# An expert queue of 71 blocks: the 38 behind the first 33 put in order by group instead of by expert

## The chip, the cores and the metric

The program runs on one core of a Trainium2 chip. A core has five engines that run at the same time, each with its own queue of instructions, taken strictly in the order written: TensorE (PE, matrix products), VectorE (DVE), ScalarE (ACT), GpSimd (POOL) and SyncE (SP, which here only starts transfers). Transfers between the on-chip memory and DRAM are started from the queues of SP, ACT and POOL and then run beside the engines. An instruction that starts a transfer waits at the head of its queue until the data that it needs are there, and everything behind it in that queue waits too. The metric is the device time of one execution in microseconds (us). "By over 0.2%" means, for this kernel, over 3.3 us.

## The reference, cut to what matters

Four layers run one after another on 64 sequences of 64 tokens, each a vector of 128 numbers: two cross-attention blocks, a gated fusion and a third attention block. The last one ends in a mixture of experts, the part that the change touches:

```python
h = _ln(x, ln_g, ln_b)
logits = h @ rw.T + rb
vals, idx = jax.lax.top_k(logits, K)          # K = 2 of E = 8 experts for each token
gates = jax.nn.softmax(vals, axis=-1)
h1 = gelu(einsum('nd,efd->enf', hf, fc1_w) + fc1_b)     # 128 -> 512
eo = einsum('enf,edf->end', h1, fc2_w) + fc2_b          # 512 -> 128
mixed = (eo[idx_f, n, :] * gates_f[..., None]).sum(axis=1)
return x + mixed
```

So each of the 4096 tokens needs the results of two experts, weighted by two gates, on top of its own row `x`.

## The kernel before, in words

**Groups.** The 4096 tokens are handled as eight groups of 512 (`NG = 8`, T = 512). A group passes through the layers as a Python generator, and `drive` (L152) interleaves the generators of several groups. The expert work, `experts` (L691), is one more generator, advanced between the others. A scheduler then fixes one order of instructions for each engine; nothing is reordered at run time.

**Router and scatter.** When a group's last attention is done, `router` (L1426) picks two experts for each token and scatters the token's row (with its number) to its place in `hrows`, a DRAM array with one region for each expert. This is 8 indirect transfers a group from POOL's queue. Region e holds the rows of expert e in the order of the groups, packed without gaps. `before` is the count of rows so far for each expert; the count after the last group of each part is kept in `endbase` (L1477, L1563).

**Blocks.** 128 rows of one region are a block, the unit of the expert queue. `PARTS = (5, 3)` splits the groups in two parts. The first part of the queue has `NSLOT[0]` = 33 blocks (L34), which are full when five groups have been routed. The second has 38. `table(h)` (L721), for the second part 34 small DVE instructions, works out on the chip which expert and which rows each block of part h has. `table(1)` walks two runs over the eight experts: first the blocks begun by the first five groups and not yet taken, then the rest. So by block 47 (`EARLY`, L35) all rows of groups 0 to 4 are done, and the blocks from 47 on have rows of groups 5, 6 and 7, expert by expert.

**One block.** `load` (L822, SP) fetches 128 rows and needs a table entry, read into a register of SP; the buffers of the rows are eight. `turn` (L844) transposes them on PE (tile `xt`) and copies them on ACT (tile `vp`); DVE works out where the result goes (`m`, `tob`). `stage_weights` (L836) copies the first weights of the block's expert on DVE (`h<-fcw`). `first` (L861) is four products on PE and the Gelu on ACT. `second` (L881) is four products on PE, one addition on DVE that takes the result out of PSUM (`km<-f,km`, called **y(i)** for block i below), and an indirect transfer on POOL that writes the rows to `yrows`. All PSUM tiles of these steps share seven buffers (`psm`).

**Sums.** `read(g)` (L909) fetches the two results of each token of a group, 256 KB each: the first (`s<-yrows`) from SP's queue, the second (`pT<-yrows`) from ACT's. A read waits for the landing of every result that may hold rows of its group. `summed(g)` (L927) is eight DVE instructions (`o<-s,gate,x` and `o<-pT,gate,o`) and one write of 256 KB from SP (`out<-o`); the tile `o` has two buffers.

**Order around the change.** The loop at L958 handles block after block: in turn t it writes `first(t)`, `second(t-2)`, `load(t+6)`, `stage_weights(t+1)` and `turn(t+2)`. L971 to L977 put in a read of groups 0 to 4 every fourth turn, the first three blocks after block 47's, each sum two turns behind its read. Groups 5, 6 and 7 are read and summed behind the last block (L979 to L985), with all three reads ahead of the first sum.

Of the kernel before, what the change touches and what calls it, by code (L numbers as in the profile page):

```python
# [13 lines left out]
ALU = mybir.AluOpType  # L14
AX = mybir.AxisListType
# [19 lines left out]
EARLY = ALL[0] + NE - 1  # L35
# [62 lines left out]
def kernel(ctx: ExitStack, tc: tile.TileContext, a: dict, out: bass.AP):  # L98
# [592 lines left out]
    def experts():  # L691
# [18 lines left out]
        def sums(nb, n, name):  # L710

            for step in (1, 2, 4, 8)[: 3 + (n > 8)]:
                more = wtile([P, 3 * NE], f"cum{step}", 1)
                nc.vector.memset(more[:, 0:NE], 0.0)
                nc.vector.tensor_tensor(
                    more[:, NE : NE + n], nb[:, NE : NE + n], nb[:, NE - step : NE - step + n], ALU.add
                )
                nb = more
            return nb[:, NE : NE + n]

        def table(h):  # L721

            ns = NSLOT[h]
            cnt = full[h] = wtile([P, NE], f"cnt{h}", 1)
            nc.vector.tensor_tensor(cnt, endbase[h], start, ALU.subtract)
            eb = wtile([P, ns], f"eb{h}", 1)
            if h == 0:
                nb = wtile([P, 3 * NE], "nb0", 1)
# [15 lines left out]

                taken = tables["taken"] = wtile([P, NE], "taken", 1)
                nc.vector.tensor_scalar(taken, cum, -1.0, float(ns), ALU.mult, ALU.add)
                nc.vector.tensor_tensor(taken, taken, whole, ALU.add)
                nc.vector.tensor_scalar(taken, taken, 0.0, None, ALU.max)
                nc.vector.tensor_tensor(taken, taken, whole, ALU.min)
                begun = tables["begun"] = wtile([P, NE], "begun", 1)  # L750
                nc.vector.tensor_reduce(begun, blocks_of(0, ALU.is_gt, 0), axis=AX.X, op=ALU.add)
            else:


                taken, begun = tables["taken"], tables["begun"]
                nb = wtile([P, 3 * NE], "nb1", 1)
                nc.vector.memset(nb[:, 0:NE], 0.0)
                at = wtile([P, 2 * NE + 1], "runs", 1)
                nc.vector.tensor_tensor(nb[:, NE : 2 * NE], begun, taken, ALU.subtract)
                late = nb[:, 2 * NE : 3 * NE]  # L760
                nc.vector.tensor_reduce(late, blocks_of(1, ALU.is_gt, 0), axis=AX.X, op=ALU.add)
                nc.vector.tensor_tensor(late, late, begun, ALU.subtract)
                cum = sums(nb, 2 * NE, "cum")
                yield
                nc.vector.scalar_tensor_tensor(
                    at[:, 0:NE], start, 1.0 / P, taken, op0=ALU.mult, op1=ALU.add
                )
                nc.vector.scalar_tensor_tensor(
                    at[:, NE : 2 * NE], start, 1.0 / P, begun, op0=ALU.mult, op1=ALU.add
                )  # L770
                nc.vector.memset(at[:, 2 * NE :], float(NE * REGION))
                step = wtile([P, 2 * NE], "step", 1)
                nc.vector.tensor_tensor(step, at[:, 1:], at[:, 0 : 2 * NE], ALU.subtract)
                nc.vector.tensor_tensor(step, step, nb[:, NE:], ALU.subtract)
                counts = wtile([P, 512], "pT", 7)
                ebs, rbs = ([counts[:, (2 * n + k) * ns : (2 * n + k + 1) * ns] for k in range(2)] for n in range(2))
                rb = counts[:, 4 * ns : 5 * ns]
                for k in range(2):
# [4 lines left out]
                    nc.vector.tensor_reduce(ebs[k], past, axis=AX.X, op=ALU.add)  # L783
                    if k == 0:

                        nc.vector.scalar_tensor_tensor(
                            eb, past[:, :, NE - 1 : NE].rearrange("p i e -> p (i e)"), -float(NE), ebs[0],
                            op0=ALU.mult, op1=ALU.add,
                        )
                    nc.vector.tensor_tensor(past, past, mid(step[:, ks], ns), ALU.mult)  # L790
                    nc.vector.tensor_reduce(rbs[k], past, axis=AX.X, op=ALU.add)
                yield
                nc.vector.tensor_tensor(eb, eb, ebs[1], ALU.add)
                nc.vector.tensor_tensor(rb, rbs[0], rbs[1], ALU.add)
                nc.vector.scalar_tensor_tensor(rb, rb, at[:, 0:1], index[:, 0:ns], op0=ALU.add, op1=ALU.add)
# [18 lines left out]
            tables[h] = tab, eb, hb  # L814

# [63 lines left out]
        results = [[] for _ in range(NH)]  # L879

        def second(i):  # L881
# [15 lines left out]
            late = i >= EARLY  # L897
            tc.add_to_no_dep_group("results", st.ins)
            if late:
                tc.add_to_no_dep_group("results1", st.ins)  # L900
            if i:
                tc.declare_no_dep(st.ins, group="results", reason="each row has one writer")
            if late and early_reads:
                tc.declare_no_dep(st.ins, group="reads0", reason="no rows of the first part in late blocks")
            results[late].append(st.ins)

        early_reads = []

        def read(g):  # L909

            h = PLACE[g][0]
            ys = []
            for k in range(2):
# [3 lines left out]
                if h == 0:  # L917
                    tc.add_to_no_dep_group("reads0", ld.ins)
                    early_reads.append(ld.ins)
                    if results[1]:  # L920
                        tc.declare_no_dep(ld.ins, group="results1", reason="no rows of the first part in late blocks")
                for st in sum(results[: h + 1], []):
                    tc.add_manual_dep(ld.ins, st.name, LANDED, reason="all results are in place")
# [715 lines left out]
```

## Time and profile before

| what | us |
|---|---|
| median of three runs | 1660.57 |
| lowest, highest | 1658.11, 1660.71 |
| the profiled execution | 1656.37 |
| its span, first to last instruction | 1654.6 |
| outside the span (difference) | 1.8 |

Times inside the kernel below are microseconds from the start of this span. The page gives the busy time of each engine and the groups of instructions; an instruction is named by its tiles, as output<-inputs, and nearly all carry the line L77, a helper through which every instruction is issued. So the reading goes by tiles. In a list of instructions by time, the number in brackets is how long the engine was idle ahead of the instruction, with what ended the wait. The granted clock is the share of full speed that TensorE was given.

| stretch of the span | what runs there |
|---|---|
| up to about 1488 | the layers, group by group |
| 1488 to 1520 | first expert blocks, beside the last scatters of rows on POOL |
| 1520 to 1637 | the rest of the 71 blocks, one every 1.9 us |
| 1637 to 1654.6 | last results land; groups 5, 6, 7 are read, summed and written |

### The profile page before, as it was taken

Reading aid. Unit: us, or ns where it says so; the run is one execution under the profiler, and the core shown is the slowest. Engines: PE = TensorE matmul, PEld = TensorE weight load, DVE = VectorE, ACT = ScalarE, POOL = GpSimd, SP = SyncE. Lnnn points to the kernel's source line nnn. Section 1 sums busy time; section 2 is a strip of 40 time slices with the busy share of each in tenths; the row PEclk is TensorE's granted clock in tenths of the full one; section 3 lists DMA queues with packets and bytes.
Section 4 is the critical chain, followed back from the end, with each engine's and each line's share of the span. In section 5 each row is a group of like instructions: output and inputs, shape, how many; then the busy total and the mean of one; then the engine's idle time right before and its main releaser. Section 6 shows DMA issues by size and latency. Waiting matters only on the chain.

```text
span 1654.6 us, 45059 instructions
## 1 busy us (share of the span) xinstructions
PE 1524.2 (92%) x17469; PEld 1132.4 (68%) x17469; DVE 1166.5 (70%) x3226; ACT 992.8 (60%) x2711; POOL 888.3 (54%) x852
## 2 busy tenths in 40 slices
PE   6999999999999999978888999989989899868995
PEld 4666666666666666646666676666767667668995
DVE  4767686867677677758897688676776688756555
ACT  4666455555655565535776565656777777427774
POOL 2546373645555564666887576644332223367543
PEclk9999999999999999979999899898999899759998
DMA  6776544545455554241001000000000000113244
GB/s 171 157 172 160 141 138 127 136 132 144 121 144 132 144 135 107 56 140 34 12 15 31 24 24 20 9 8 8 2 2 15 21 2 7 35 54 86 74 116 125
DMA packets 215540, 131.40 MB, mean 79 GB/s; under 512 B 38416, under 2 KB 201490, under 8 KB 215328
## 3 DMA queue, kind: packets, MB, share of 16 engines
q1 hardware_dynamic: 186016, 90.52, 22.9%
q10 hardware_dynamic: 24992, 29.54, 5.7%
q0 software_dynamic: 4320, 8.47, 1.5%
q8 instruction: 139, 2.28, 0.6%
q14 instruction: 73, 0.60, 0.1%
HBM read 66.48 MB, written 62.47 MB: 78 GB/s over the span
## 4 chain that ended last, share of the span: by engine, by line
PE 65%; DVE 18%; ACT 6%; POOL 6%; DMA 3%; issue 2%; SPq 0%; ACTq 0%; DVEq 0%; POOLq 0%
PE av L77 8%; PE psv L77 8%; PE proj L77 7%; PE psk L77 6%; PE f L77 6%; PE pt L77 6%; PE tok L77 5%; DVE mx L77 4%; PE pbd L77 4%; DVE s L77 4%; PE psc L77 4%; PE acc L77 3%; PE tr L77 2%; ACT z L77 2%; PE sc L77 2%
## 5 line engine op out<-in xcount | busy, mean ns | idle before, releaser
L77 ACT ACTIVATE s<-s,nm 128x128 f32<-128x128 f32 x512 | 198.1, 388 | 236.8 <-DVE nm L77 220.5
L77 POOL TENSOR_TENSOR s<-s,sm 128x512 f32<-128x512 f32 x128 | 130.4, 1040 | 208.7 <-DVE sm L77 208.7
L77 PE MATMUL pt<-ident,s 128*128 128x128 f32 x1536 | 213.0, 282 | 19.3 <-DVE s L77 12.1
L77 POOL TENSOR_TENSOR s<-s,mx 128x512 f32<-128x512 f32 x160 | 164.4, 1046 | 99.8 <-DVE mx L77 93.6
L77 PEld LDWEIGHTS pt<-ident,s 128*128 128x128 f32 x1536 | 177.0, 145 | 41.2 <-issue 17.7
L77 POOL TENSOR_TENSOR skew<-skew,mb 128x512 f32<-128x512 f32 x128 | 159.9, 1270 | 70.7 <-DMA skew<-scr 70.2
L77 ACT ACTIVATE pT<-pt 128x512 f32<-128x512 f32 x256 | 140.5, 600 | 79.6 <-PE pt L77 71.3
L77 POOL TENSOR_TENSOR rs<-rs,nhalf 128x4 f32<-128x4 f32 x72 | 73.3, 1018 | 151.9 <-DVE rs L77 144.1
L77 PEld LDWEIGHTS av<-vb,pT 128*64 128x64 f32 x4096 | 132.2, 143 | 23.4 <-issue 12.4
L77 PE MATMUL av<-vb,pT 128*64 128x18 f32 x4096 | 140.4, 215 | 6.8 <-DVE o L77 4.8
L77 DVE TENSOR_REDUCE mx<-s 128x8 f32<-128x512 f32 x160 | 102.8, 675 | 40.1 <-ACT s L77 40.1
L77 PE MATMUL psv<-wv,kv 128*128 128x256 f32 x512 | 127.4, 392 | 0.0
L77 PE MATMUL psk<-kv,wk 128*128 128x512 f32 x256 | 127.0, 618 | 0.0
L77 PE MATMUL sc<-km,qs 32*64 32x256 f32 x2048 | 106.3, 422 | 8.9 <-ACT qs L77 4.4
L77 DVE COPY pT<-pt 128x512 f32<-128x512 f32 x128 | 82.0, 681 | 36.9 <-PE pt L77 36.9
L77 PEld LDWEIGHTS psv<-wv,kv 128*128 128x128 f32 x512 | 92.2, 189 | 15.1 <-issue 1.0
L77 PEld LDWEIGHTS pbd<-rT,qp 64*128 64x128 f32 x1024 | 62.1, 187 | 58.3 <-DVE qp L77 56.5
L77 PEld LDWEIGHTS av<-pT,v 128*64 128x64 f32 x2048 | 66.8, 138 | 50.9 <-issue 31.3
L77 DVE TENSOR_TENSOR s<-sc,mb 128x512 f32<-128x512 f32 x128 | 82.4, 680 | 25.0 <-PE sc L77 25.0
L77 POOL DMA_INDIRECT yrows<-km,tob x71 | 71.2, 1004 | 53.1 <-DVE tob L77 26.4
L77 DVE TENSOR_TENSOR s<-psc,skew 128x512 f32<-128x512 f32 x128 | 87.4, 683 | 13.9 <-issue 6.3
L77 ACT ACTIVATION_READ_ACCUMULATOR s<-s,nm 128x1 f32 x512 | 95.6, 187 | 0.0
(256 smaller groups left out, 3523.3 us busy)
## 6 DMA issues: line engine op xcount, KB each, us to landing
scr<-stage SPq DMA_DIRECT2D x64, 516.0 KB, 4.8
skew<-scr SPq DMA_DIRECT2D x128, 256.0 KB, 4.3
hrows<-pad ACTq DMA_DIRECT2D x53, 325.0 KB, 2.5
ctx<-in_ctxT SPq DMA_DIRECT2D x24, 256.0 KB, 2.6
km<-hrows SPq DMA_DIRECT2D x71, 65.0 KB, 2.0
fcw<-in_fc ACTq DMA_DIRECT2D x16, 256.0 KB, 4.0
kv<-in_xT SPq DMA_DIRECT2D x8, 256.0 KB, 4.9
kv<-in_ctxT SPq DMA_DIRECT2D x8, 256.0 KB, 5.4
```

The lines of the kernel that those rows point to most:

```text
L77: ins = it(*args, **kw)
```

## The change

The second part of the queue is no longer ordered by two runs over the experts but by four (`LEVELS`), so 32 runs in all: first the blocks begun by groups 0 to 4, then those begun by group 5, by group 6, and by group 7. The number of blocks stays 71. From `BOUNDS`, the results of groups 0 to 4 are complete with block 46, of group 5 with block 54, of group 6 with block 62 and of group 7 with block 70. `table(1)` therefore works out the blocks begun after each of these groups and goes through four rounds of comparisons in place of two, and through five steps of prefix sums over 32 entries in place of four over 16. `router` keeps the counts after each of the last four groups (`ends_of`). In `table(0)` the instructions that only `table(1)` needs are written behind the rest.

`SUMS` puts the read of group g at block 50 + 3g (50, 53, 56, 59, 62, 65, 68 for groups 0 to 6), two turns ahead of its sum. Only group 7 is read and summed behind the last block. The declarations of which writes and reads of `yrows` are independent follow the four levels.

```diff
-EARLY = ALL[0] + NE - 1
+
+
+LEVELS = NG - PARTS[0] + 1
+BOUNDS = [2 * (PARTS[0] + k) * T // P + NE - 1 for k in range(LEVELS)]
+SUMS = [max(BOUNDS[0] + 3 + 3 * g, BOUNDS[max(g - PARTS[0] + 1, 0)] + 3) for g in range(NG - 1)]
...
-            for step in (1, 2, 4, 8)[: 3 + (n > 8)]:
-                more = wtile([P, 3 * NE], f"cum{step}", 1)
+            for step in (1, 2, 4, 8, 16)[: 3 if n == NE else 5]:
+                more = wtile([P, (LEVELS + 1) * NE], f"cum{step}", 1)
+                cut = max(step - NE, 0)
                 nc.vector.memset(more[:, 0:NE], 0.0)
+                if cut:
+                    nc.vector.tensor_copy(more[:, NE : NE + cut], nb[:, NE : NE + cut])
                 nc.vector.tensor_tensor(
-                    more[:, NE : NE + n], nb[:, NE : NE + n], nb[:, NE - step : NE - step + n], ALU.add
+                    more[:, NE + cut : NE + n], nb[:, NE + cut : NE + n],
+                    nb[:, NE + cut - step : NE + n - step], ALU.add,
                 )
                 nb = more
...
+                n = LEVELS * NE
+                nb = wtile([P, (LEVELS + 1) * NE], "nb1", 1)
+                nc.vector.memset(nb[:, 0:NE], 0.0)
+                at = wtile([P, n + 1], "runs", 1)
+                prev = tables["taken"]
+                for k in range(LEVELS):
+                    ks, ns1 = slice(k * NE, (k + 1) * NE), slice((k + 1) * NE, (k + 2) * NE)
+                    nc.vector.scalar_tensor_tensor(at[:, ks], start, 1.0 / P, prev, op0=ALU.mult, op1=ALU.add)
+                    if k == 0:
+                        begun = tables["begun"]
+                    else:
+                        full[1] = wtile([P, NE], "cnt1", 1)
+                        nc.vector.tensor_tensor(full[1], ends_of[PARTS[0] - 1 + k], start, ALU.subtract)
+                        begun = wtile([P, NE], f"begun{k}", 1)
+                        nc.vector.tensor_reduce(begun, blocks_of(1, ALU.is_gt, 0), axis=AX.X, op=ALU.add)
+                    nc.vector.tensor_tensor(nb[:, ns1], begun, prev, ALU.subtract)
+                    prev = begun
+                    yield
+                cum = sums(nb, n, "cum")
+                yield
+                nc.vector.memset(at[:, n:], float(NE * REGION))
+                step = wtile([P, n], "step", 1)
+                nc.vector.tensor_tensor(step, at[:, 1:], at[:, 0:n], ALU.subtract)
+                nc.vector.tensor_tensor(step, step, nb[:, NE:], ALU.subtract)
+                counts = wtile([P, 512], "pT", 7)
+                sb, sr, rb = (counts[:, k * ns : (k + 1) * ns] for k in range(3))
+                nc.vector.tensor_scalar(rb, index[:, 0:ns], at[:, 0:1], None, ALU.add)
+                for k in range(LEVELS):
+                    yield
+                    past = v3(wtile([P, 512], "pT", 7)[:, 0 : ns * NE], ns)
+                    ks = slice(k * NE, (k + 1) * NE)
+                    nc.vector.tensor_tensor(past, last(index[:, 0:ns], NE), mid(cum[:, ks], ns), ALU.is_ge)
+                    nc.vector.tensor_reduce(sb if k else eb, past, axis=AX.X, op=ALU.add)
+                    if k:
+                        nc.vector.tensor_tensor(eb, eb, sb, ALU.add)
+                    if k + 1 < LEVELS:
+
+                        nc.vector.scalar_tensor_tensor(
+                            eb, past[:, :, NE - 1 : NE].rearrange("p i e -> p (i e)"), -float(NE), eb,
+                            op0=ALU.mult, op1=ALU.add,
+                        )
+                    nc.vector.tensor_tensor(past, past, mid(step[:, ks], ns), ALU.mult)
+                    nc.vector.tensor_reduce(sr, past, axis=AX.X, op=ALU.add)
+                    nc.vector.tensor_tensor(rb, rb, sr, ALU.add)
...
-                nc.vector.tensor_reduce(late, blocks_of(1, ALU.is_gt, 0), axis=AX.X, op=ALU.add)
-                nc.vector.tensor_tensor(late, late, begun, ALU.subtract)
-                cum = sums(nb, 2 * NE, "cum")
...
-                for k in range(2):
-                    yield
-                    past = v3(wtile([P, 512], "pT", 7)[:, 0 : ns * NE], ns)
-                    ks = slice(k * NE, (k + 1) * NE)
-                    nc.vector.tensor_tensor(past, last(index[:, 0:ns], NE), mid(cum[:, ks], ns), ALU.is_ge)
-                    nc.vector.tensor_reduce(ebs[k], past, axis=AX.X, op=ALU.add)
-                    if k == 0:
-
-                        nc.vector.scalar_tensor_tensor(
-                            eb, past[:, :, NE - 1 : NE].rearrange("p i e -> p (i e)"), -float(NE), ebs[0],
-                            op0=ALU.mult, op1=ALU.add,
-                        )
-                    nc.vector.tensor_tensor(past, past, mid(step[:, ks], ns), ALU.mult)
-                    nc.vector.tensor_reduce(rbs[k], past, axis=AX.X, op=ALU.add)
...
+            level = max(g - PARTS[0] + 1, 0)
+            early_reads.add(level)
             ys = []
             for k in range(2):
                 y = wtile([P, NBLK, D], ("s", "pT")[k], (10, 7)[k])
                 at = k * B * S + g * T
                 ld = (nc.sync, nc.scalar)[k].dma_start(y, yrows[at : at + T, :].rearrange("(k p) d -> p k d", p=P))
-                if h == 0:
-                    tc.add_to_no_dep_group("reads0", ld.ins)
-                    early_reads.append(ld.ins)
-                    if results[1]:
-                        tc.declare_no_dep(ld.ins, group="results1", reason="no rows of the first part in late blocks")
-                for st in sum(results[: h + 1], []):
+                tc.add_to_no_dep_group(f"reads{level}", ld.ins)
+                if len(results) > BOUNDS[level]:
+                    tc.declare_no_dep(
+                        ld.ins, group=f"late{level}", reason="no rows of the level's groups in later blocks"
+                    )
+                for st in results[: BOUNDS[level]]:
                     tc.add_manual_dep(ld.ins, st.name, LANDED, reason="all results are in place")
...
-            for h in range(NH - 1):
-                g, at = divmod(t - 2 - EARLY - 3, 4)
-                if 0 <= g < PARTS[0]:
-                    if at == 0:
-                        reads[g] = read(g)
-                    if at == 2:
-                        summed(g, reads.pop(g))
-            yield
-        rest = range(NG - PARTS[-1], NG)
-        for g in rest[:3]:
-            reads[g] = read(g)
-        for g in rest:
-            if g + 3 < NG:
-                reads[g + 3] = read(g + 3)
-            summed(g, reads.pop(g))
+            for g in range(NG - 1):
+                at = t - 2 - SUMS[g]
+                if at == 0:
+                    reads[g] = read(g)
+                if at == 2:
+                    summed(g, reads.pop(g))
+            yield
+        summed(NG - 1, read(NG - 1))
...
-                    h, gl = PLACE[g]
-                    dst = endbase[h] if gl == PARTS[h] - 1 else wtile([P, NE], "base", 2)
+                    dst = ends_of[g] if g in ends_of else wtile([P, NE], "base", 2)
                     bases[g + 1] = dst
```

## The prediction

> **What bounds the kernel now.** The busy times of the page come first (PE 1524.2 us, 92%), but the change sits in the last 150 us, so the windows of that stretch decide, and then the lists by time. Columns of the windows: length, busy time and instructions of each engine, granted clock, DMA share, GB/s.
>
> ```profile
> 1600.00:1620.00 20.00, 20.00 (x182) 20.00 (x181) 12.74 (x53) 16.32 (x55) 9.97 (x10) 1.00 0.57 158
> 1620.00:1640.00 20.00, 16.73 (x149) 16.35 (x147) 12.03 (x43) 11.81 (x39) 12.29 (x13) 0.98 0.34 96
> 1640.00:1655.00 15.00, 0.00 (x0) 0.00 (x0) 6.49 (x24) 0.00 (x0) 0.00 (x0) 0.50 0.58 158
> ```
>
> PE is full through the blocks, at a granted clock of 1.00 and 1.90 us a block, and stands still for the last 15 us. The chain of the end (start, length) tells what that tail is made of:
>
> ```profile
> 1638.12 2.11 DMA yrows<-km,tob
> 1640.43 3.75 DMA s<-yrows
> 1644.28 0.49 DVE o L77 x2
> ```
>
> Last result landed by 1640.4, first pair read 3.85 us later, then 24 DVE instructions for three groups. The change takes two of the three groups out of this tail. So the question is what putting them among the blocks costs. SP's queue and DVE's waits show how the five early groups go there today:
>
> ```profile
> 1606.23 0.40 SPq L77 DMA_DIRECT2D out<-o  x1
> 1607.35 1.33 SPq L77 DMA_DIRECT2D km<-hrows  x2
> 1608.77 0.38 SPq L77 DMA_DIRECT2D s<-yrows  x1
> ...
> 1628.45 0.38 SPq L77 DMA_DIRECT2D out<-o  x1
> 1628.93 0.48 SPq L77 DMA_DIRECT2D s<-yrows  x1
> ```
>
> ```profile
> 1603.82 0.61 DVE L77 SCALAR_TENSOR_TENSOR o<-s,gate,x 128x128 f32<-128x128 f32 x2 [1.49 <-DMA s<-yrows]
> ...
> 1620.04 0.61 DVE L77 SCALAR_TENSOR_TENSOR o<-s,gate,x 128x128 f32<-128x128 f32 x2 [0.28 <-DMA s<-yrows]
> ...
> 1626.03 0.61 DVE L77 SCALAR_TENSOR_TENSOR o<-s,gate,x 128x128 f32<-128x128 f32 x2 [0.40 <-DMA s<-yrows]
> ...
> 1631.86 0.63 DVE L77 SCALAR_TENSOR_TENSOR o<-s,gate,x 128x128 f32<-128x128 f32 x2 [0.26 <-DMA s<-yrows]
> ...
> 1636.77 0.29 DVE L77 TENSOR_TENSOR km<-f,km 128x128 f32<-128x128 f32 x1 [0.60 <-PE f L77]
> ```
>
> A group is a loop through two queues: the read on SP, 3.0 us to landing, the sum on DVE, its write on SP, and only behind that write the next read. The sums from 1620.04 on stand 5.99 and 5.83 us apart, and DVE waited for the read each time. The last line is the last block's addition.
>
> **The change part by part.** All sums use the profiled execution: 1656.37 us, 1.8 of it outside the span. It lies 4.2 us (0.25%) below the median 1660.57, so I carry the difference over to the median.
>
> *The tail.* Were nothing else late, the tail would be one pair (3.0 us alone, 1628.93 to 1631.86; 3.85 with six reads in flight; I take 3.5), one sum (1648.90 to 1651.09: 2.2) and 3.5 from its end to the span's end (1651.09 to 1654.6): 1640.4 + 3.5 + 2.2 + 3.5 = 1649.6, a gain of 5.0 us.
>
> *Seven groups through the same loop.* In the order built for the changed kernel, SP's queue still holds read, write, read, write in strict turn: one row load stands between write and next read for groups 1 to 3, none for groups 4 to 7. The sums are placed every three blocks (5.7 us). The loop needs: read to sum 3.0 (2.93 to 3.09); sum to write 2.4 (1603.82 to 1606.23); write to read 0.48, or with one load about 1.6 (1.12 to the load, and a third to a half of the two loads' 1.33; 1.5 to 1.8). That is 7.0 with a load and 5.9 without. From group 0's sum at 1603.8, which nothing in this part moves, the sums start at 1610.8, 1617.8, 1624.8, 1630.7, 1636.6 and 1642.5 (group 6). Three blocks of other work would have put group 6 at 1638. What queues behind that wait: DVE's order has the first instruction of group 6's sum ahead of y(70), the last block's addition, which is ready at 1636.77 today. It becomes 1642.8. POOL then sends the result (0.6 to 0.7 later, as 1631.30 to 1631.90), it lands 2.3 after that (1638.12 to 1640.43), at 1645.8. Group 7's read: + 3.5 + 2.2 + 3.5 = 1655.0. Against 1654.6 that is **+0.4**: the loop gives back the 5.0. Group 6's write is issued at about 1645, before that read, and costs nothing.
>
> By the Trainium skill ("DMA: Bandwidth & Descriptors", section Anatomy of one DMA) a transfer takes 2.0 us and its bytes over 436 GB/s, an estimate of 2.6 us for 256 KB where the rows say 3.0. Six loops would then be 2.4 us shorter in all and the tail -2.0 in place of +0.4; the measured rows decide.
>
> *Two more waits on ACT.* The second reads of groups 5 and 6 stand in ACT's queue right behind the Gelu of blocks 57 and 65, and wait for the results of blocks 54 and 62. Group 0's read stands just so today: in the lists by time ACT's Gelu at 1597.12 had waited 2.46 us for yrows, and PE at 1598.66 0.76 for ACT.
>
> The loop delays y(54) and y(62) by some 3 and 5 us, so I estimate ACT waits of about 3 us and PE stalls of 2 to 3 us each. PE would then finish at about 1641.6 (1636.7 + 5), still ahead of the 1642.5 above: they cost nothing while the loop is later, and up to 1 us if it is not. Bounds 0 and +1.
>
> *The longer table(1).* 64 DVE instructions in place of 34: two more whole-block comparisons (0.43 + 0.41 each), two more rounds of four 304-element instructions (0.47, 0.46, 0.43, 0.46), the rest at 0.07 to 0.2. By the distance to the next start about 6 us more. Does DVE have them? PE can't start block t before y(t-5) has freed a PSUM buffer; two rows show it, block 11 behind y(6) and block 12 behind y(7):
>
> ```profile
> 1515.84 1.13 PE L77 MATMUL f<-vp,h 128*128 128x128 f32 x8 [0.94 <-DVE m L77]
> 1516.80 1.06 PE L77 MATMUL f<-fcw,s 128*128 x8
> 1520.25 0.33 PE L77 MATMUL xt<-ident,km 128*128 128x128 f32 x1 [2.39 <-DVE km L77]
> ```
>
> A block without table work costs DVE 1.27 us (additions at 1530.54 and 1531.81 in its list) of PE's 1.90. Today the table lies between y(6) and y(12), and y(8) to y(12) take 1521.77 to 1529.26, 1.87 a block: DVE just keeps up. In the built order the new table spreads to y(17): adding its instructions block by block, y(16) ends at 1537.0, needed at 1537.6, y(17) at 1539.1, needed at 1539.5. Covered by about 0.5 us; where the cover is short, each further microsecond is paid in full, up to 6. And y(7) stands behind one table instruction instead of four after the wait that ends at 1518.7, so PE restarts 0.7 earlier. I take 0 for the two together; bounds -0.7 and +6.
>
> *table(0) and the scatters.* POOL sends row scatters back to back (1.26 us each) until 1515, with two gaps. In the new DVE order a copy that waits for PE (`mb<-pb`) stands ahead of the addresses (`to`, 1482.44) of group 5's first scatters: eight 0.25 us passes of `pb` and the copy make them about 1.3 later. The second gap, 1.40 where 0.30 is usual, swallows 1.1 of it: +0.3; bounds -1 and +1.3.
>
> **Sum:** +0.4 + 0 + 0 + 0.3 = +0.7 us. The profiled execution would be 1657.1, the median **1661.3**.
>
> **The rivals.**
> *Faster: the loop doesn't bind.* y(70) stays at about 1637 and the 5.0 us are kept: -5.0 + 0.3 gives 1655.9. It decides if a loop takes no more than three blocks, 5.7 us. For it: sums of groups 1 and 2 in today's trace hardly waited. Against: they stand four blocks apart, and where they come closer, 5.8 to 6.0 was the least.
> *Slower: table(1) starves PE.* The price is at most the 6 us, with the sum 1667.3; half of it, 1664.3. It decides once DVE is over 0.5 us later than worked out at block 16 or 17. For it: today's 1.87 a block is already at the limit. Against: the new instructions are spread wider.
> *It doesn't do what it says:* group 5 or 6 read behind the last block after all. The built order speaks against it; by the loop the time would hardly differ.
>
> **How the numbers follow.** The loop case 0.60, its own range 1658.5 to 1664 (six loops at 0.3 us each, and the ACT and scatter bounds); the faster rival 0.14; starved PE or a slower loop 0.26. Three runs before spread over 2.6 us. For 8 in 10 I reach from 1656.5, most of the way to the faster case, to 1666.5, nearly the whole price of the table. 3.3 us either way is about what a measurement tells from no change: faster 0.14, same 0.60, slower 0.26.
>
> **What would show it.** Right: reads on SP each directly behind a write, six or more sums that waited for `s<-yrows`, sums 5.9 to 7.0 us apart, group 6's near 1642 in the clock of before, y(70) 5 to 6 us after PE's last product could have let it go, and a tail from y(70) to the end of about 12 us, where 17.8 stood. Wrong: sums 5.7 us apart with short waits and y(70) behind PE at once (faster); PE idle behind DVE around blocks 14 to 22 (slower); a wait for yrows on ACT that ends later than group 6's read. A wrong latency is multiplied by six, so that is the likeliest error of size.

## The result

The changed kernel takes 1665.67 us (median of 20 runs, 1657.46 to 1668.39), the kernel before 1660.45 (20 runs beside them, 1656.93 to 1664.69). The ratio is 1.0026, with a 95% interval from 1.0015 to 1.0037: slower by 4.3 us (2.5 to 6.1); the medians themselves lie 5.2 us apart. Taking two of three groups out of the tail did not pay. The prediction had 1661.3 and a range from 1656.5 to 1666.5. The time lies in the range, but 4.4 us above the number, and the slowdown of 0.26% is just past the 0.2% that was to count as no difference.

The profiled execution of the changed kernel took 1666.99 us, its span 1665.2, which is 10.6 us longer than the span before. Most of that stands ahead of the changed part. The last load of `ctx`, which both kernels issue long before the second table is worked out, starts at 1328.6 where it started at 1320.3. In the 14 profiles of this study it starts between 1319.8 and 1328.6, and two profiles of one and the same kernel differ there by 4.0. So stretches are compared from here on, not times from the start. The mark is the addition of block 30 on DVE, y(30) in the prediction's words, which lies in the even part of the blocks (1562.01 before, 1570.12 after: 8.1 later, about as much as at the load of `ctx`).

| stretch, us | before | after |
|---|---|---|
| last `ctx` load to y(30) | 241.7 | 241.6 |
| y(30) to y(70), the last block's addition | 74.8 | 82.8 |
| y(70) to the end of the span | 17.8 | 12.3 |
| y(30) to the end | 92.6 | 95.1 |

The tail is 5.6 us shorter, as the change wants it, and the blocks ahead of it are 8.1 us longer.

Busy time in the last stretches of the changed kernel comes first, 8 us later than in the table before (columns: length, busy time and instructions of PE, weight loads, DVE, ACT and POOL, granted clock, DMA share, GB/s).

```profile
1608.00:1628.00 20.00, 16.08 (x139) 15.88 (x139) 13.35 (x55) 12.51 (x43) 9.32 (x9) 0.97 0.62 164
1628.00:1648.00 20.00, 19.77 (x167) 19.54 (x166) 11.58 (x45) 13.65 (x47) 8.40 (x9) 0.94 0.41 115
1648.00:1665.00 17.00, 2.53 (x23) 2.34 (x21) 6.00 (x22) 1.03 (x4) 4.85 (x5) 0.68 0.36 98
```

PE was full in the first of these stretches before; now 4 of 20 us are idle there, nearly all of it one wait of 3.92 us for ACT, which in turn waits to issue group 5's second read. The granted clock is lower too, and it is so right behind that wait:

```profile
1627.00:1630.00 3.00, 3.00 (x16) 3.00 (x15) 1.87 (x9) 1.54 (x6) 1.72 (x2) 0.50 0.42 111
1631.00:1634.00 3.00, 3.00 (x29) 3.00 (x28) 2.23 (x10) 2.49 (x9) 0.98 (x1) 1.00 0.33 103
```

At 0.50 PE has 16 products in 3 us, at 1.00 it has 29. SP's queue shows the loop (start, length, instruction):

```profile
1635.09 0.40 SPq L81 DMA_DIRECT2D out<-o  x1
1635.59 0.45 SPq L81 DMA_DIRECT2D s<-yrows  x1
1641.08 0.38 SPq L81 DMA_DIRECT2D out<-o  x1
1641.83 0.96 SPq L81 DMA_DIRECT2D s<-yrows  x1
1648.49 0.38 SPq L81 DMA_DIRECT2D out<-o  x1
1649.56 0.36 SPq L81 DMA_DIRECT2D s<-yrows  x1
1655.21 0.38 SPq L81 DMA_DIRECT2D out<-o  x1
1655.92 0.36 SPq L81 DMA_DIRECT2D s<-yrows  x1
```

Every read starts behind the write of the group before it, never earlier. On DVE the loop shows first in another way than forecast. The sums of groups 1, 2 and 3 start without any wait for their read; for groups 1 and 2 it is a block's rows that DVE waited for just ahead (1.38 and 1.63 us), and SP had issued the load of these rows behind the same write (1614.31 and 1621.50). Group 1:

```profile
1616.88 0.21 DVE L81 TENSOR_SCALAR m<-km,eb 128x1 f32<-128x1 f32 x1 [1.38 <-DMA km<-hrows]
...
1617.96 0.61 DVE L81 SCALAR_TENSOR_TENSOR o<-s,gate,x 128x128 f32<-128x128 f32 x2
```

The sums of groups 4 to 7 do wait for their reads, 0.22, 3.08, 2.71 and 4.20 us. DVE, in order of time:

```profile
1638.67 0.61 DVE L81 SCALAR_TENSOR_TENSOR o<-s,gate,x 128x128 f32<-128x128 f32 x2 [0.22 <-DMA s<-yrows]
...
1642.71 0.29 DVE L81 TENSOR_TENSOR km<-f,km 128x128 f32<-128x128 f32 x1 [1.03 <-PE f L81]
1646.08 0.61 DVE L81 SCALAR_TENSOR_TENSOR o<-s,gate,x 128x128 f32<-128x128 f32 x2 [3.08 <-DMA s<-yrows]
1647.14 0.28 DVE L81 TENSOR_TENSOR km<-f,km 128x128 f32<-128x128 f32 x1
...
1648.39 0.68 DVE L81 TENSOR_TENSOR km<-f,km 128x128 f32<-128x128 f32 x2
1649.67 0.29 DVE L81 TENSOR_TENSOR km<-f,km 128x128 f32<-128x128 f32 x1 [0.60 <-PE f L81]
1652.67 0.35 DVE L81 SCALAR_TENSOR_TENSOR o<-s,gate,x 128x128 f32<-128x128 f32 x1 [2.71 <-DMA s<-yrows]
1652.94 0.28 DVE L81 TENSOR_TENSOR km<-f,km 128x128 f32<-128x128 f32 x1
```

1646.08 is group 5's sum. DVE waited 3.08 us for its read, and y(66) stands behind it, at 1647.14; y(67) and y(68) follow at once, y(69) as soon as PE lets it go. 1652.67 is group 6's first instruction, with 2.71 us of waiting, and behind it y(70). The chain that ended last (start, length, engine or transfer):

```profile
1637.59 3.22 DMA yrows<-km,tob
...
1640.99 0.43 ACTq L81
...
1643.01 2.05 PE f L81 x16
...
1645.17 3.59 PE f L81 x32
...
1648.78 0.30 DVE km L81
...
1650.39 0.98 POOL yrows L81
...
1653.50 2.21 DMA yrows<-km,tob
...
1655.92 3.44 DMA s<-yrows
```

This chain does not go through group 5's sum. It goes back from y(68) over PE to ACT, which waited for the result of block 62 to issue group 6's second read. But POOL's queue joins it to the loop. POOL stood idle for 3.44 us until y(66), behind group 5's sum, let it send at 1647.70; from there it sends one result after another, 1.28 us each, and y(68), ready at 1649.1, goes out at 1650.39. y(70) comes 0.5 us too late for its turn, because of group 6's first instruction. The last result lands at 1655.71, and only then group 7 is read. Group 6's write, the loop's own last step, is issued at 1655.21, so it would hold that read nearly as long. Several paths end here within 0.5 us of each other, and one profile can't tell what the time would be without one of them; the experiments can.

### The profile page after: what moved, and what is told of

Same layout as the page of the kernel before. It is cut to its first block, busy times and chain, and to the rows that moved or that the text cites. A ratio compares the mean times of both kernels' runs of the same rounds, so it can differ in the third digit from the quotient of the medians.

```text
span 1665.2 us, 45103 instructions
## 1 busy us (share of the span) xinstructions
PE 1532.9 (92%) x17469; PEld 1140.9 (69%) x17469; DVE 1172.5 (70%) x3254; ACT 993.0 (60%) x2711; POOL 889.2 (53%) x852
## 4 chain that ended last, share of the span: by engine, by line
PE 63%; DVE 19%; POOL 6%; ACT 5%; issue 3%; DMA 3%; POOLq 0%; ACTq 0%; DVEq 0%; SPq 0%
PE av L81 8%; PE psv L81 8%; PE proj L81 7%; PE psk L81 7%; PE pt L81 6%; DVE mx L81 5%; PE pbd L81 4%; PE tok L81 4%; PE f L81 4%; DVE s L81 4%; PE psc L81 4%; PE acc L81 3%; PE tr L81 3%; PE sc L81 2%; ACT z L81 2%
## 5 line engine op out<-in xcount | busy, mean ns | idle before, releaser
L81 PE MATMUL pt<-ident,s 128*128 128x128 f32 x1536 | 215.5, 284 | 19.6 <-DVE s L81 12.6
L81 POOL TENSOR_TENSOR s<-s,mx 128x512 f32<-128x512 f32 x160 | 164.3, 1046 | 98.9 <-DVE mx L81 92.6
```

The source lines that it names most:

```text
L81: ins = it(*args, **kw)
```

## The experiments

The theory is that of the prediction, *the loop*: seven groups go through read on SP, sum on DVE, write on SP, next read, and that loop sets the end. Its rivals: the longer table costs the time; ACT's waits for the second reads do, by holding PE; the place of y(70) in DVE's queue does; or the difference is the scatter of the early part. The kernels ran on chips on which the kernel before has different medians: 1696.22 and 1695.34 us on chip B (two sittings), 1662.53 on chip C, 1657.04 on chip D, against 1660.45 where the result was measured, called A here. Ratios are to runs of the kernel before on the same chip in the same sitting; us in brackets behind a ratio are that ratio on the median. Each stretch comes from one profiled execution.

| kernel | chip | ratio, 95% interval | y(30) to y(70) | y(70) to end | y(30) to end |
|---|---|---|---|---|---|
| before | A | | 74.8 | 17.8 | 92.6 |
| after | A | 1.0026 (1.0015 to 1.0037) | 82.8 | 12.3 | 95.1 |
| before again | B | | 76.3 | 18.3 | 94.6 |
| after again | B | 1.0032 (1.0009 to 1.0056) | 84.6 | 12.1 | 96.6 |
| table only | B | 1.0009 (0.9988 to 1.0029) | 77.3 | 17.9 | 95.2 |
| ACT freed | B | 1.0021 (1.0000 to 1.0041) | 84.7 | 12.6 | 97.3 |
| reads ahead | B | 0.9981 (0.9957 to 1.0004) | 78.1 | 13.4 | 91.4 |
| reads ahead | D | 0.9993 (0.9980 to 1.0006) | 77.5 | 13.5 | 91.0 |
| reads ahead, ACT freed | B | 1.0001 (0.9977 to 1.0026) | 75.2 | 13.8 | 89.0 |
| the same again | B | 0.9987 (0.9963 to 1.0010) | 75.5 | 13.8 | 89.4 |
| y(70) first | C | 1.0010 (0.9997 to 1.0024) | 82.6 | 14.7 | 97.3 |
| all three | B | 0.9973 (0.9951 to 0.9994) | 77.2 | 13.8 | 91.0 |
| all three | D | 0.9968 (0.9954 to 0.9983) | 74.1 | 13.6 | 87.7 |
| before, reads ahead | C | 0.9988 (0.9975 to 1.0001) | 74.9 | 18.0 | 92.9 |

### Both kernels again, on one chip

No edit.

> The kernel before, unchanged, for a second profile, taken on the same chip as the three that follow. If the lead of 8 us that the profile of the kernel before had over the changed one ahead of all changed work (both at the same instructions) is scatter between executions, then on one chip the two differ there by less than 5 us or with the other sign; the stretch from the addition of block 30 to the end is again about 92.6 us.

> The changed kernel, unchanged, on the same chip. If the result is a property of the changed stage: about 95 us from the addition of block 30 to the end, sums 7.0 to 7.5 us apart for groups 1 to 3 and 6 to 7.4 from there, the last block's addition behind the first instruction of group 6's sum, and 2 to 5 us above the kernel before. If the 4.3 us came from the early part, the stretch is within 1 us of the kernel before's 92.6.

At the last load of `ctx` the two differ by 3.5 us (1322.7 and 1326.2), less than 5. From y(30) to the end they take 94.6 and 96.6. The number for the kernel before was missed by 2 us (chip B is slower here too), the difference was not: +2.0, where chip A had +2.5. The sums of the changed kernel start 7.1, 7.4, 7.9, 6.0, 7.1 and 6.6 us apart, and y(70) again comes right behind group 6's first instruction. The whole program is slower by 5.4 us here (1.5 to 9.5). So most of the 8 us of the first pair of profiles ahead of the change were scatter. Not all need be: the kernel before starts that load at 1319.9 to 1322.7 in its three profiles, the changed kernel and its variants at 1319.8 to 1328.6 in eleven, and a small difference would be hidden in this. The 2 to 2.5 us behind y(30) were there both times and are put down to the change.

### The table and the order of blocks alone

```diff
-            for g in range(NG - 1):
-                at = t - 2 - SUMS[g]
+            for g in range(PARTS[0]):
+                at = t - 2 - BOUNDS[0] - 3 - 4 * g
...
-        summed(NG - 1, read(NG - 1))
+        rest = range(PARTS[0], NG)
+        for g in rest:
+            reads[g] = read(g)
+        for g in rest:
+            summed(g, reads.pop(g))
...
-            level = max(g - PARTS[0] + 1, 0)
+            level = (LEVELS - 1) * (g >= PARTS[0])
```

> The table of 32 runs and the new order of blocks stay, but the reads and sums are placed as before: groups 0 to 4 every four blocks from block 50, groups 5, 6 and 7 read behind the last block, all three reads ahead of their sums. Loop theory (the time comes from seven groups going through read, sum, write, read): the table costs about nothing, so the time is that of the kernel before within 1.5 us (0.2 to 0.5 us for the scatters), the sums of groups 0 to 4 stand as before, and the tail from the last addition to the end is again about 17.8 us. Table theory (the longer table or what it moves costs the time): it stays 3 us or more above the kernel before, with PE idle behind DVE around blocks 11 to 22.

Ratio 1.0009, +1.5 us (-2.0 to +4.9), which alone leaves both theories standing. The stretches decide: 95.2 us against 94.6 of the kernel before on that chip, with the tail of 17.9 back. PE waited nowhere for DVE in the last 100 us. So table and order cost at most some 0.6 us there. What they cost ahead of y(30) is in the stretch from the last `ctx` load to y(30) on the chips where it is steady: 241.7 (before) and 241.6 (after) on A, 242.0 twice on D with the new table. No cost shows there.

### The second reads of groups 5 and 6 from SP: ACT freed

```diff
-                ld = (nc.sync, nc.scalar)[k].dma_start(
+                ld = (nc.sync if g in (5, 6) else (nc.sync, nc.scalar)[k]).dma_start(
...
+                if k and g in (5, 6):
+                    tc.add_manual_dep(ld.ins, first_ld.name, mybir.DependencyInfo(mybir.DependencyClass.NoSync, mybir.DependencyReason.DATA))
+                first_ld = ld.ins
```

The last lines fix an order without adding a wait: the second read directly behind the first on SP.

> The changed kernel with one thing moved: the second reads of groups 5 and 6 are issued from SP, directly behind the first reads, instead of from ACT, so ACT and PE no longer wait for the results of blocks 54 and 62. Loop theory: the PE stall of 3.9 us behind ACT goes, but the sums still set the end, so the time is within 1 us of the changed kernel. ACT theory (the stall of PE is what costs): it falls 3 to 4 us, to about the kernel before.

97.3 us against 96.6, and 3.6 us above the kernel before (0 to 7.0): taking ACT's waits away gains nothing, though the granted clock stays at 1.00 to PE's last product in this profile. The sums still start 7.1, 7.6, 7.0, 6.0, 6.4 and 6.9 us apart. DVE in this kernel, around group 5's and group 6's sum:

```profile
1674.52 1.14 DVE L81 SCALAR_TENSOR_TENSOR o<-s,gate,x 128x128 f32<-128x128 f32 x4 [3.16 <-DMA s<-yrows]
1675.58 0.28 DVE L81 TENSOR_TENSOR km<-f,km 128x128 f32<-128x128 f32 x1
1676.83 0.68 DVE L81 TENSOR_TENSOR km<-f,km 128x128 f32<-128x128 f32 x3
1681.37 0.35 DVE L81 SCALAR_TENSOR_TENSOR o<-s,gate,x 128x128 f32<-128x128 f32 x1 [3.86 <-DMA s<-yrows]
```

PE no longer waits for ACT where groups 5 and 6 are read. It waits for DVE instead, whose additions stand behind the sums (the longest two, in groups 2's and 3's):

```profile
1656.26 0.33 PE L81 MATMUL xt<-ident,km 128*128 128x128 f32 x1 [1.18 <-DVE km L81]
...
1663.28 0.33 PE L81 MATMUL xt<-ident,km 128*128 128x128 f32 x1 [0.64 <-DVE km L81]
```

And the chain that ended last now goes through the reads of groups 3, 5 and 7:

```profile
1659.11 2.94 DMA s<-yrows
...
1671.32 3.12 DMA s<-yrows
...
1684.68 3.64 DMA s<-yrows
```

So ACT's waits were covered by the loop, as forecast.

### The next read ahead of the write: the loop broken

```diff
-                if at == 2:
+                if at == 4:
                     summed(g, reads.pop(g))
             yield
-        summed(NG - 1, read(NG - 1))
+        reads[NG - 1] = read(NG - 1)
+        for g in sorted(reads):
+            summed(g, reads.pop(g))
...
+            if g + 1 < NG:
+                tc.add_manual_dep(wr.ins, firsts[g + 1].name, mybir.DependencyInfo(mybir.DependencyClass.NoSync, mybir.DependencyReason.DATA))
```

`wr` is the write of group g, `firsts[g + 1]` the first read of the next group. The last two lines put the write behind that read on SP, again without a wait. The first lines place each sum two blocks later, so DVE's order changes with SP's.

> The changed kernel with one thing turned round: on SP's queue the first read of group g+1 stands ahead of the write of group g, so a read no longer waits for the sum before it. Loop theory: sums are no longer 7.2 us apart, the last block's addition comes 4 to 8 us earlier, and the time falls 4 to 8 us below the changed kernel, that is from 0 to 4 us below the kernel before. Theory that the loop is only a bystander (the time comes from ACT's waits for the second reads, from the table, or from the early part): within 1.5 us of the changed kernel, about 5 us above the kernel before.

91.4 us against 96.6 of the changed kernel and 94.6 of the kernel before: 5.2 us off the stretch. The time is 3.2 us below the kernel before (-7.3 to +0.7), and its ratio 0.9981 (0.9957 to 1.0004) lies below the changed kernel's 1.0032 (1.0009 to 1.0056) with no overlap. This is the experiment that the loop theory stands on. It doesn't tell how much is due to SP's order and how much to the later place of the sums on DVE: no variant has one without the other. Once more on chip D:

> The changed kernel with the reads ahead of the writes alone, once more. Here ACT still issues the second reads of groups 5 and 6. If ACT's waits begin to count as soon as the loop is broken: PE stalls 1 to 4 us behind ACT around block 57, and the stretch is 1.5 to 3 us longer than in the variant with these reads on SP, 91 to 92 us; the time is 0 to 3 us below the kernel before. If ACT's waits never count: 89 to 90 us, as with the reads on SP.

91.0 us and 1.2 us below the kernel before (-3.3 to +1.0), as expected. y(30) to y(70) is still 2.7 us longer than before on chip A, and the list of PE names the main reason, which the loop had hidden:

```profile
1617.70 1.16 PE L81 MATMUL f<-vp,h 128*128 128x128 f32 x8 [2.13 <-ACT vp L81]
```

### Both turns

The edit is the sum of the two above.

> Both: reads ahead of writes on SP, and the second reads of groups 5 and 6 from SP. Loop theory, with ACT's waits as what comes next once the loop is broken: 1 to 3 us below the variant with the reads ahead alone, so 2 to 5 us below the kernel before, which is most of the 5.0 us that two groups less in the tail can bring. If neither loop nor ACT waits matter: within 1.5 us of the changed kernel.

> Reads ahead of writes on SP, and the second reads of groups 5 and 6 from SP, once more, on the same chip as the changed kernel itself. Loop theory, with the stretch measured once as 89.0 us from the addition of block 30 to the end: 88 to 90 again, so 5 to 7 us below the changed kernel and 2 to 5 below the kernel before. If the first stretch was chance: within 2 us of the changed kernel.

The stretch is 89.0 and 89.4 us, about 2 us below the variant with the reads ahead alone and 7.4 below the changed kernel. So ACT's waits cost nothing beside the loop and about 2 us without it, by these four profiles; the scatter of such stretches is not much smaller (89.0 to 91.0 on chip B with ACT freed, if the kernel with all three turns is counted in). The time of the whole program tells less on this chip: ratios 1.0001 and 0.9987, intervals from 0.9963 to 1.0026; the first missed its expectation and the second met it only in part (-2.2 us, -6.3 to +1.7).

### The last addition ahead of group 6's sum, in the changed kernel

```diff
+                if g == NG - 2:
+                    tc.add_manual_dep(step.ins, adds[-1].name, mybir.DependencyInfo(mybir.DependencyClass.NoSync, mybir.DependencyReason.DATA))
```

`step` is each first-read instruction of group 6's sum, `adds[-1]` is y(70).

> The changed kernel with the addition of the last block put ahead of all of group 6's sum on DVE; the loop of read, sum, write stays. Loop theory: the addition comes 2 to 3 us earlier, but the read of group 7 still stands behind the write of group 6 on SP, and that write waits for the sum that the loop holds; so the stretch from the addition of block 30 to the end stays within 1 us of the changed kernel's 95.1 to 96.6 us. Theory that the place of the last addition in DVE's queue is what costs (as the prediction's chain has it): the stretch falls by 2 to 3 us, to 93 to 94.

The stretch is 97.3 us, not below 95.1 to 96.6: this place in the queue is not the cause. But the expectation was wrong in one point: y(70) did not come earlier (82.6 us behind y(30), 82.8 before the turn). The last lines of DVE and POOL:

```profile
1649.21 0.29 DVE L81 TENSOR_TENSOR km<-f,km 128x128 f32<-128x128 f32 x1 [0.60 <-PE f L81]
```

```profile
1650.34 0.98 POOL L81 DMA_INDIRECT yrows<-km,tob  x1 [0.31 <-issue]
1651.62 0.98 POOL L81 DMA_INDIRECT yrows<-km,tob  x1 [0.30 <-issue]
```

The time is 1.7 us above the kernel before (-0.5 to +4.0). y(70) waits for PE here, and PE is late itself: it stood 4.29 us behind ACT for group 5's second read, and ran at a granted clock of 0.50 behind that. From y(70)'s start to its send it takes another 2.4 us, since POOL's queue is still at the results before; that queue began at 1646.35, behind group 5's sum (1644.74, after a wait of 2.73 for its read) and y(66). The end is the loop's. In this profile the chain that ended last runs through the reads of groups 5, 6 and 7, each behind the write of the group before:

```profile
1640.80 3.84 DMA s<-yrows
...
1648.21 3.01 DMA s<-yrows
...
1654.23 3.95 DMA s<-yrows
```

### The three turns together, and a control

> The same, and the addition of the last block ahead of all of group 6's sum on DVE. In the profile of the variant without this it came 0.34 us plus one instruction of 0.34 late, so 0.5 to 1 us below that variant; with the loop broken nothing else can be gained by this order. If the queueing of the last addition on DVE were itself the main cause, and not the loop that holds the sum, the gain here would be 3 us or more.

> The changed kernel with all three turns (next read ahead of the write on SP, second reads of groups 5 and 6 from SP, the last block's addition ahead of group 6's sum), once more on another chip. Loop theory: 89 to 91 us from the addition of block 30 to the end, and 2 to 5 us below the kernel before. If the first measurement was chance: within 1.5 us of the kernel before.

Chip B: ratio 0.9973, -4.6 us (-8.3 to -1.0), though its stretch of 91.0 is longer than the 89.4 without the third turn: PE stood 1.1, 1.0 and 0.45 us behind ACT in that profile, 0.4 and 0.8 in the other. The gain of the third turn by itself can't be told. Chip D: ratio 0.9968, -5.3 us (-7.6 to -2.8), and 87.7 us for the stretch. Both intervals lie below the kernel before, and the one of chip B also below the changed kernel's; on chip D the changed kernel was not run. On SP, reads stand ahead of writes (chip D):

```profile
1620.29 0.38 SPq L81 DMA_DIRECT2D s<-yrows  x1
1620.76 0.46 SPq L81 DMA_DIRECT2D out<-o  x1
1621.32 0.45 SPq L81 DMA_DIRECT2D s<-yrows  x1
1626.00 0.38 SPq L81 DMA_DIRECT2D out<-o  x1
1626.75 0.36 SPq L81 DMA_DIRECT2D s<-yrows  x1
```

The sums of groups 0 to 5 start 5.4, 5.3, 5.5, 5.1 and 4.6 us apart, and y(70) waits for nothing but PE (this kernel, chip D, DVE; the last line is group 7's sum):

```profile
1640.38 0.29 DVE L81 TENSOR_TENSOR km<-f,km 128x128 f32<-128x128 f32 x1 [0.60 <-PE f L81]
...
1648.34 0.61 DVE L81 SCALAR_TENSOR_TENSOR o<-s,gate,x 128x128 f32<-128x128 f32 x2 [5.57 <-DMA s<-yrows]
```

The control turns reads and writes of groups 0 to 4 in the kernel before, by the same edit:

> The kernel before, with the same turn on SP's queue as in the variants of the changed kernel: for groups 0 to 4 the next read stands ahead of the write. Groups stand four blocks apart there and three groups are read behind the last block in any case. Loop theory: the turn breaks the same loop, but nothing that sets the end waits on it, so the time and the stretch from the addition of block 30 to the end (92.6 and 94.6 us) stay within 1 us. Theory that the turn is good in itself (less waiting on SP anywhere): 2 us or more below the kernel before.

92.9 us from y(30) to the end, against 92.6 on chip A. Its ratio 0.9988 (0.9975 to 1.0001) can't tell 0 from 2 us, so the stretch has to decide, and it shows no change. The loop costs only where the end depends on it.

## Why the prediction came out as it did

**The tail: right.** "Were nothing else late", two groups fewer gain 5.0 us. With all three turns the stretch on chip D is 87.7 where the kernel before has 92.6 on A and 92.9 on C: about 5 us; on chip B it is 89.0 to 91.0 where 94.6 stood. The remaining tail was forecast as about 12 us from y(70) on; it is 12.3.

**The loop: the mechanism right, its size wrong.** This is the term that was mis-sized. It had 7.0 us a group with a row load and 5.9 without, 38.7 from group 0's sum to group 6's; the profile has 41.9, 3.2 more. By pair of groups (sum, write, next read, next sum in the lists of the changed kernel):

| from group to group | 0-1 | 1-2 | 2-3 | 3-4 | 4-5 | 5-6 |
|---|---|---|---|---|---|---|
| forecast | 7.0 | 7.0 | 7.0 | 5.9 | 5.9 | 5.9 |
| sum to write | 2.41 | 2.41 | 2.41 | 2.41 | 2.41 | 2.41 |
| write to read | 1.58 | 1.56 | 1.57 | 0.50 | 0.75 | 1.07 |
| read to sum | 3.21 | 3.46 | 3.31 | 3.08 | 4.25 | 3.11 |
| all | 7.20 | 7.43 | 7.29 | 5.99 | 7.41 | 6.59 |

Sum to write was right, and write to read was right for groups 1 to 4. Read to sum was taken as 3.0 (2.93 to 3.09). It was 3.1 for groups 4 and 6, and 4.25 for group 5, whose read started 0.8 us behind group 6's second read, issued by ACT at 1640.99. In the kernel that issues that second read from SP, behind it, group 5's took 3.20. So the nearer row was that of the old tail, 3.85 with several reads in flight; the trace of before has an even slower one that the working passed over, group 0's, issued at 1598.62 among five reads from ACT and waited for until 1603.82, 5.2 us. The 3.2 to 3.5 of groups 1 to 3 are not the reads' time, since DVE did not wait for them: DVE came to these sums only then, behind a block's rows or PE. So the sign "six or more sums that waited" came for four, and up to group 3 the loop runs through the row loads behind the write, and through PE's stall, as much as through the reads. For groups 5 and 6 write to read was 0.75 and 1.07 in place of 0.48, and much the same in the other variants that keep the order on SP (0.75 and 1.20 with ACT freed). These two reads also wait for the results of their own level, those of groups 1 to 4 do not. SP's trace has five wait instructions between write and read for groups 5 and 6, 0.06 to 0.07 us apart for group 5, where it has one for group 4. That this is the reason was not tried by itself. Groups 5 and 6 alone are 2.2 of the 3.2. Group 0's sum came 1.2 us earlier than forecast. Net 2.0, and with the +0.4 of the prediction's sum that is 2.4 of the measured 2.5.

The Trainium skill ("DMA: Bandwidth & Descriptors", section Anatomy of one DMA) would give 2.6 us for a read of 256 KB, as an estimate; the section is headed for transfers from GpSimd, and these reads are issued by SP. The rows in which DVE waited for the read show 3.1 to 4.3 from read to sum, so the estimate lies further off than the prediction's row did. The same section says that a wait for a semaphore is made by the sequencer that issues the transfer, before it is sent off. SP's list agrees: no read starts ahead of the write before it in the queue, and the variant with the two turned, and the sums two blocks later, took 5.2 us off the stretch with no wait taken away.

**Where the loop meets the end: half right.** The prediction let the loop act on y(70), behind group 6's first instruction. y(70) does stand there, but the experiment with y(70) first gained nothing, and it came only 2.4 us after PE's last product (1650.53), not the 5 to 6 us that the prediction measured from a PE on time. The loop acts through group 5's sum as well: y(66) stands behind it, and POOL's sends of 1.28 us each keep the later results waiting. Also "group 6's write ... costs nothing" does not hold: the last result lands at 1655.71 and that write is issued at 1655.21, so either alone would hold group 7's read to within 0.5 us. With y(70) first, the chain goes through group 6's sum and, behind its write, group 7's read.

**ACT's two waits: right while the loop is there, too small without it.** PE was held 3.9 us for group 5 (forecast 2 to 3) and 0.2 for group 6; freeing ACT gained nothing while the loop was there. PE's last products began at 1650.3, which is 1642.2 in the clock of before (1641.6 forecast). "Up to 1 us" with the loop gone was too small: about 2. One part of the price was not in the working: behind the stall PE ran at half the clock. Of the fourteen profiles, four have a granted clock of 0.50 somewhere between y(30) and PE's last product, for 3 us or more: those in which PE had just waited 3.92, 3.84, 4.29 and 2.45 us for ACT (the changed kernel twice, y(70) first, reads ahead on B). Reads ahead on D, with 2.13 us, kept 1.00. An estimate from the 16 and 29 products above: 3 us at half the clock cost PE about 1.3 us.

**Table and scatters: nearly right.** PE's restart, with the later stalls and the wait on ACT beside it:

```profile
1527.55 0.33 PE L81 MATMUL xt<-ident,km 128*128 128x128 f32 x1 [1.82 <-DVE km L81]
1530.09 0.33 PE L81 MATMUL xt<-ident,km 128*128 128x128 f32 x1 [0.42 <-DVE km L81]
1532.60 1.13 PE L81 MATMUL f<-vp,h 128*128 128x128 f32 x8 [0.28 <-DVE m L81]
...
1625.72 1.16 PE L81 MATMUL f<-vp,h 128*128 128x128 f32 x8 [3.92 <-ACT vp L81]
```

The stall of 2.39 us became 1.82, 0.42 and 0.28, together 2.5, and nothing over 0.3 follows until block 57. The one ahead of it grew from 0.94 to 1.61, so PE did not restart 0.7 earlier; the two together cost 0.8 where 0 was taken, but the stretch from `ctx` to y(30) is no longer for it. POOL's first gap became 1.2 us longer and the second went from 1.40 to 0.30, as worked out. The slower rival, starved PE, had 64 instructions and a thin cover for it, and did not come.

**The chances.** The case with the most chance, the loop, is what happened, with an error that the prediction named as its likeliest, a wait that counts once for each group. But the stretch behind y(30) is only 2.5 us longer, or 0.15%, which by itself is "same"; what carries the time past 0.2% is a rest that no run explains. The time even lies above the loop case's own range, which ended at 1664; the whole range holds it because its upper end was set by the price of the table, which did not come. That is luck. Of the slowdown of the whole program, 4.3 us on chip A and 5.4 on B, the stretches show 2.5 and 2.0. The rest, some 2 to 3.5 us, is within what the intervals allow; whether it is chance (the runs of one kernel spread over 7 to 18 us) or something that these profiles do not show stays open.

## What to carry to other kernels

When work is moved from a tail into a busy stretch, follow every queue that it passes: here a read issued behind a write, which waits for a sum, which waits for the read before, was a loop of 6 to 7.4 us a group in the changed kernel, and its length times the number of groups decided here, not the work. Put the next read ahead of the write in the queue before such work is moved; in the kernel where it was not needed no cost showed. And price a read by rows in which other reads of its size are in flight, where they will be, not by one that runs alone.

## What had not been expected of the hardware

On chip B the same programs take about 35 us longer, and 33 of them lie between the last load of `ctx` and y(30): 274.8 us for the kernel before, 241.7 on chip A. DVE's list of the kernel before on chip B has two waits there, of 8.9 and 8.7 us, whose end the profile can't name ("remote"); the first:

```profile
1529.92 0.43 DVE L77 COPY h<-fcw 128x512 f32 x1 [8.86 <-remote]
```

On chip A that kernel has no such wait for "remote". In the six profiles on chips A, C and D this stretch is 241.6 to 244.7 us, on chip B it is 275 or 281, also for one kernel run twice (280.8 and 275.5). What it is was not settled; it lies ahead of the stretch that the experiments compare.

The issue of a read on SP took 0.36 to 0.45 us in most cases. Group 5's took 0.96, 0.78 and 0.87 in the three profiles of the changed kernel and of y(70) first, in which ACT had issued group 6's second read about 1 us before, and 0.36 where that read had been moved to SP. But group 2's took 0.68 to 1.12 in these four profiles, with no read from ACT just ahead of it. Why was not tried.
